# Moving a convolution-weight transform from the head of a kernel to beside its first attention

## The chip, the cores and the metric

The kernel runs on one core of a Trainium2 chip. The metric is the device time of one execution in microseconds (us). The profile is one execution recorded by the hardware profiler; "the trace" is the record of its single instructions. TensorE does matrix products (PE in the profile; PEld is its weight load), VectorE is DVE, ScalarE is ACT, GpSimd is POOL, and SyncE (SP) here only issues transfers.

## The reference, cut to what matters

The program is two layers on four images of 128 channels and 64x64 pixels ("sequences" of 4096 positions). Only the first layer is touched by the change:

```python
x = x + conv_block(group_norm(x))        # first layer
# conv_block(x) = relu(conv7(x) + conv5(x) + conv3(x) + nonlocal(x) + x), all fp32
# nonlocal: theta, phi, g = three 1x1 projections; softmax(theta^T phi / 8) applied to g; 1x1 projection
# second layer: a two-directional state-space block and a recurrence on 4 x 4096 tokens (untouched)
```

The three convolutions and the identity are merged into one 7x7 kernel, which is brought into a form with fewer products: each of the seven kernel rows is turned into ten 128x128 matrices ("the transform", tensor `u`), and the padded image `xp` into matching combinations of every fourth column ("strips", tensors `f` and `x`).

## The kernel before: the parts that matter

```python
def conv_attention(nc, tc, k, a, t, dmax, B, H, W):
    ...
    for h in range(2):                      # small weights, behind the whole input on SyncE's queue
        nc.sync.dma_start(tw2[:, h, :], a["tpw"][:, 0:IC]); ...      # pw2, tb2, ow2
    nc.sync.dma_start(gw, a["gwt"]); nc.sync.dma_start(gb, a["gb"])
    for i, name in enumerate(("b7", "b5", "b3", "ob")):
        nc.sync.dma_start(bias[:, i : i + 1], a[name])
    ...
    nc.vector.tensor_reduce(bsum, bias, AX.X, ALU.add)               # the bias sum
    with tc.tile_pool(name="l0_ws", bufs=2) as ws:
        for y in range(7):
            conv_weights(nc, ws, k, a, u, y)                         # the transform, row by row
    fp = ctx.enter_context(tc.tile_pool(name="l0_fir", bufs=2))      # the strips take its space
    for b in range(B):
        # statistics of the sequence (st), group norm (pm, gm, dm, qv, pv, ve, rs), normed image xp
        # projections theta, phi, gT
        # attention: 128 steps of two score matmuls (pf), exponential (ex), den += ex, two value matmuls (acc)
        # convolution: strips f and x from xp, products with u
        ...

def load():                                 # whole sequences
    for b in range(B):
        nc.sync.dma_start(t[:, b * T : (b + 1) * T], a["x"][b].rearrange("c h w -> c (h w)"))
```

The framework that builds the program ("the build" below) does not keep the source's order on an engine: an instruction may be put into an earlier gap, as the strips in the prediction's last lines of VectorE are.

Of the kernel before, what the change touches and what calls it, by code (L numbers as in the profile page):

```python
# [15 lines left out]
P = 128  # L16
# [6 lines left out]
IC = 64  # L23
# [72 lines left out]
def conv_attention(nc, tc, k, a, t, dmax, B, H, W):  # L96
# [18 lines left out]
    with ExitStack() as ctx:  # L115
# [10 lines left out]
        bsum = wp.tile([P, 1], F32, name="bsum")  # L126
        for h in range(2):
            half = slice(h * IC, (h + 1) * IC)
            nc.sync.dma_start(tw2[:, h, :], a["tpw"][:, 0:IC])
            nc.sync.dma_start(pw2[:, h, :], a["tpw"][:, IC:P])  # L130
            nc.sync.dma_start(tb2[half], a["tb"])
            nc.sync.dma_start(ow2[half], a["owt"])
        tw2, pw2 = (w.rearrange("p h c -> p (h c)") for w in (tw2, pw2))
        nc.sync.dma_start(gw, a["gwt"])
        nc.sync.dma_start(gb, a["gb"])
        for i, name in enumerate(("b7", "b5", "b3", "ob")):
            nc.sync.dma_start(bias[:, i : i + 1], a[name])
        wk = ctx.enter_context(tc.tile_pool(name="l0_wk", bufs=2))
        xpp = ctx.enter_context(tc.tile_pool(name="l0_xp", bufs=1))
        big = ctx.enter_context(tc.tile_pool(name="l0_big", bufs=1))  # L140
# [7 lines left out]
        nc.tensor.matmul(pgb, ow2[0:IC], gb, start=True, stop=True)  # L148
        nc.vector.tensor_tensor(bsum, bsum, pgb, ALU.add)

        with tc.tile_pool(name="l0_ws", bufs=2) as ws:
            for y in range(7):
                conv_weights(nc, ws, k, a, u, y)
        fp = ctx.enter_context(tc.tile_pool(name="l0_fir", bufs=2))
        xtp = ctx.enter_context(tc.tile_pool(name="l0_pt", bufs=4))

        pe = InOrder(tc, nc.tensor)
        for b in range(B):
# [112 lines left out]
                        divide(q - 1)  # L271
            divide(NQ - 1)


            att = theta.rearrange("p (r w) -> p r w", w=W)

# [72 lines left out]
    return c  # L349


def conv_weights(nc, ws, k, a, u, y):

    w = ws.tile([P, 7, P], F32, tag="w", name="w")
    nc.scalar.dma_start(w, a["w7t"][:, y * 7 : (y + 1) * 7, :])
    for n in (5, 3):
        m = (7 - n) // 2
        if m <= y < 7 - m:
            v = ws.tile([P, n, P], F32, tag=f"v{n}", name="v")
            nc.scalar.dma_start(v, a[f"w{n}t"][:, (y - m) * n : (y - m + 1) * n, :])  # L360
            nc.vector.tensor_tensor(w[:, m : 7 - m, :], w[:, m : 7 - m, :], v, ALU.add)
    if y == 3:

        nc.vector.scalar_tensor_tensor(w[:, 3, :], k.ident, 2.0, w[:, 3, :], ALU.mult, ALU.add)
    nc.vector.tensor_scalar(u[:, 0, y, :], w[:, 0, :], 1.0 / poly(POINTS)[0], None, ALU.mult)
    nc.vector.tensor_copy(u[:, 1, y, :], w[:, 6, :])
    for n, p in enumerate(POINTS):
        c = 0.5 / p**2
        for r in POINTS[:n] + POINTS[n + 1 :]:
            c /= p**2 - r**2  # L370
        part = []
        for odd in range(2):
            s = ws.tile([P, P], F32, tag=f"s{odd}", name="s")
            nc.vector.tensor_scalar(s, w[:, odd, :], c * p**odd, None, ALU.mult)
            for j in range(odd + 2, 7, 2):
                nc.vector.scalar_tensor_tensor(s, w[:, j, :], c * p**j, s, ALU.mult, ALU.add)
            part.append(s)
        nc.vector.tensor_tensor(u[:, 2 + 2 * n, y, :], part[0], part[1], ALU.add)
        nc.vector.tensor_tensor(u[:, 3 + 2 * n, y, :], part[0], part[1], ALU.subtract)


def conv_attention_general(nc, tc, k, a, t, B, H, W):
# [760 lines left out]
@with_exitstack  # L1143
def kernel(ctx: ExitStack, tc: tile.TileContext, a: dict, out: bass.AP):
    nc = tc.nc
    B, C, H, W = out.shape
    T = H * W
    cpool = ctx.enter_context(tc.tile_pool(name="const", bufs=1))
    t = cpool.tile([P, B * T], F32, name="t")
    o = out.rearrange("b c h w -> c b (h w)")  # L1150

    def load():
        for b in range(B):
            nc.sync.dma_start(t[:, b * T : (b + 1) * T], a["x"][b].rearrange("c h w -> c (h w)"))

    load()
    k = Consts(nc, cpool)
    dmax = cpool.tile([P, B * (T // NC)], F32, name="dmax")
    flags = cpool.tile([P, 2], F32, name="flags")
    conv_attention(nc, tc, k, a, t, dmax, B, H, W)  # L1160
    nc.vector.tensor_reduce(flags[:, 0:1], dmax, AX.X, ALU.max)
    nc.vector.tensor_scalar(flags[:, 0:1], flags[:, 0:1], DEN_MAX, None, ALU.is_gt)
    mamba(nc, tc, k, a, t, B, T)
    recurrence(nc, tc, k, a, t, flags[:, 1:2], o, B, T)

    n = cpool.tile([1, 1], mybir.dt.int32, name="nflags")
    with tc.tile_pool(name="ps_flags", bufs=1, space=PSUM) as ps:
        pn = ps.tile([1, 2], F32, name="pflags")
        nc.tensor.matmul(pn, k.ones[:, 0:1], flags, start=True, stop=True)
        nf = cpool.tile([1, 1], F32, name="nf")  # L1170
        nc.vector.tensor_reduce(nf, pn, AX.X, ALU.add)
        nc.vector.tensor_copy(n, nf)
    again = nc.values_load(n[0:1, 0:1], min_val=0, max_val=2 * P, skip_runtime_bounds_check_because="a count of flags")
    with tc.If(again > 0):
        load()
        conv_attention_general(nc, tc, k, a, t, B, H, W)
        mamba(nc, tc, k, a, t, B, T)
        recurrence(nc, tc, k, a, t, None, o, B, T)
# [42 lines left out]
```

## Time and profile before

| | us |
|---|---|
| median of three runs (lowest, highest) | 3421.4 (3418.4, 3432.1) |
| first score matmul (the attention of sequence 1 begins) | 115.0 |
| end of the first attention (first product of the convolution) | 366.9 |
| first score matmul of sequence 2 | 545.2 |

The first stage, up to the second sequence's first score, can be read from single instructions; the rest of the program (2864 to 2882 us in the traces here) is the same code in every kernel below and merely starts earlier or later. The lines of the profile on which the argument rests are in the prediction.

### The profile page before, as it was taken

The numbers are of one execution on the slowest core, as the hardware profiler recorded it, in microseconds if no ns is written. First come the engines' busy times: TensorE is split into PE (matmuls) and PEld (weight loads), VectorE is DVE, ScalarE is ACT, GpSimd is POOL, SyncE is SP. The second block draws the span as 40 slices with busy tenths as digits, with TensorE's granted clock in tenths as the row PEclk, the third lists the DMA queues.
The fourth block names the chain that finished last, engine by engine and source line by source line (L and its number), as shares of the span: only waits on it lengthen the run. The fifth ranks groups of instructions, "written<-read, shape, count | busy, mean of one in ns | idle before, by whom it ended". The sixth has DMA issues, their size and how long they took to land.

```text
span 3409.2 us, 44429 instructions
## 1 busy us (share of the span) xinstructions
PE 2991.7 (88%) x16048; PEld 1445.4 (42%) x16048; DVE 2708.1 (79%) x4682; ACT 1726.3 (51%) x3047; POOL 529.2 (16%) x735
## 2 busy tenths in 40 slices
PE   0899998999989999899996888888888898888776
PEld 0233343333433334233343555555555565555446
DVE  8977858778587785877856998899889988898755
ACT  0445204452045420344204777677777767777454
POOL 0000000000000000000000443244324332334310
PEclk9999999999999999999996999999999999999888
DMA  4000000000000000000002332333233233333002
GB/s 165 1 1 1 0 1 1 1 1 0 0 1 1 1 0 0 1 1 1 0 0 52 77 82 75 78 75 84 67 80 80 76 75 78 84 81 78 2 1 101
DMA packets 72437, 128.21 MB, mean 38 GB/s; under 512 B 16912, under 2 KB 20240, under 8 KB 71184
## 3 DMA queue, kind: packets, MB, share of 16 engines
q1 hardware_dynamic: 65664, 115.63, 13.0%
q10 hardware_dynamic: 6544, 9.65, 0.8%
q8 instruction: 129, 2.11, 0.3%
q14 instruction: 100, 0.82, 0.1%
HBM read 115.80 MB, written 9.44 MB: 37 GB/s over the span
## 4 chain that ended last, share of the span: by engine, by line
PE 57%; DVE 27%; ACT 5%; issue 4%; POOL 3%; DMA 2%; SPq 0%; ACTq 0%; DVEq 0%; POOLq 0%
PE pf L91 14%; PE acc L91 13%; PE pr L286 11%; DVE xx L754 5%; PE pc L286 3%; DVE bc L754 3%; DVE cbc L840 2%; ACT xx L91 2%; DVE y L877 2%; DVE f L298 2%; DVE xdt L833 2%; DVE xdd L833 2%; PE pj L892 1%; POOL xx L91 1%; PE pys L857 1%
## 5 line engine op out<-in xcount | busy, mean ns | idle before, releaser
L233 ACT ACTIVATE ex<-pf 128x1024 f32<-128x1024 f32 x512 | 496.7, 1021 | 495.8 <-PE pf L91 487.3
L237 DVE TENSOR_TENSOR den<-den,ex 128x1024 f32<-128x1024 f32 x448 | 547.1, 1221 | 209.5 <-ACT ex L233 184.7
L91 PE MATMUL pf<-theta,phi 64*128 64x512 f32 x2048 | 509.3, 615 | 1.8 <-ACT ex L233 1.8
L91 PE MATMUL acc<-ex,gT 128*64 128x512 f32 x2048 | 501.2, 606 | 0.0
L286 PE MATMUL pr<-x,u 128*128 128x512 f32 x896 | 386.3, 593 | 0.0
L91 PEld LDWEIGHTS pf<-theta,phi 64*128 64x128 f32 x2048 | 175.7, 186 | 328.4 <-ACT ex L233 186.8
L91 ACT ACTIVATE cbc<-cbc,s 128x128 f32<-128x128 f32 x1024 | 312.9, 406 | 0.0
L91 PEld LDWEIGHTS acc<-ex,gT 128*64 128x64 f32 x2048 | 121.9, 136 | 344.8 <-issue 343.7
L286 PEld LDWEIGHTS pr<-x,u 128*128 128x128 f32 x896 | 170.0, 190 | 219.3 <-issue 216.0
L754 DVE SCALAR_TENSOR_TENSOR xx<-pj,cw,xx 128x509 f32<-128x509 f32 (+2 forms) x384 | 259.6, 735 | 0.4
L857 PE MATMUL pys<-cbc,xdt 128*64 128x128 f32 x2048 | 180.5, 296 | 81.7 <-DVE y L877 81.6
L91 POOL TENSOR_TENSOR rms<-rms,neghalf 128x2 f32<-128x2 f32 x128 | 113.3, 885 | 569.7 <-DVE rms L903 569.7
L327 ACT COPY m<-pr 128x512 f32<-128x512 f32 x32 | 18.8, 586 | 356.5 <-PE pr L286 356.5
L91 ACT ACTIVATE cbc<-cbc 128x1536 f32<-128x1536 f32 x128 | 190.0, 1485 | 3.4
L298 DVE SCALAR_TENSOR_TENSOR f<-xp,f 128x1120 f32<-128x1120 f32 x88 | 190.7, 2180 | 1.0
L91 POOL TENSOR_TENSOR y<-y,zs 128x512 f32<-128x512 f32 x128 | 163.4, 1276 | 147.0 <-DVE y L877 144.5
L857 PEld LDWEIGHTS pys<-cbc,xdt 128*64 128x64 f32 x2048 | 115.9, 142 | 145.1 <-DVE y L877 110.6
L745 PE MATMUL pj<-un,full 128*128 128x512 f32 x256 | 147.4, 661 | 33.8 <-DVE xx L754 19.5
L767 PE MATMUL pj<-un,full 128*128 128x512 f32 x256 | 146.0, 677 | 32.9 <-DVE xx L754 18.0
L91 ACT ACTIVATE xx<-pj,cb,cw 128x512 f32<-128x512 f32 x128 | 97.6, 774 | 144.9 <-DVE y L877 104.9
L892 PEld LDWEIGHTS pj<-wout,y 128*128 128x128 f32 x1024 | 133.4, 199 | 59.1 <-issue 48.5
L181 POOL MEMSET xp<- 128x210 f32 x4 | 1.1, 274 | 1011.4 <-DVE f L298 1011.4
(210 smaller groups left out, 4991.1 us busy)
## 6 DMA issues: line engine op xcount, KB each, us to landing
cbc<-csd SPq DMA_DIRECT2D x256, 256.0 KB, 4.4
cbc<-csd SPq DMA_DIRECT2D x256, 128.0 KB, 4.5
t<-in_x SPq DMA_DIRECT2D x4, 2048.0 KB, 11.8
out<-t SPq DMA_DIRECT2D x2, 2048.0 KB, 18.5
out<-t ACTq DMA_DIRECT2D x2, 2048.0 KB, 18.8
w<-in_w7t ACTq DMA_DIRECT2D x7, 448.0 KB, 8.5
v<-in_w5t ACTq DMA_DIRECT2D x5, 320.0 KB, 14.3
csd<-cs SPq DMA_DIRECT2D x16, 64.0 KB, 1.6
```

What stands on the lines that cost most here:

```text
L91: return self.tc.keep_in_program_order(getattr(self.engine, name)(*args, **kw))
L233: nc.scalar.activation(ex, pf, AF.Exp, scale=scale)
L237: nc.vector.tensor_tensor(den[q], exs[q, 0] if m == 1 else den[q], ex, ALU.add)
L286: nc.tensor.matmul(o, u[:, n, y, :], x[:, q * QR + y : q * QR + y + QR, :], start=(y == 0), stop=(y == 6 and odd is None),)
L298: nc.vector.scalar_tensor_tensor(f, strip(i + 2 * j), cs[j], f, ALU.mult, ALU.add)
L745: pe.matmul(pp, full[:, d, DI + h * P : DI + (h + 1) * P], own(un, d, g), start=True, stop=True)
L754: vec.scalar_tensor_tensor(x[:, o:], self.pp[i][:, 0 : MG - o], cw[:, i, tap : tap + 1], x[:, o:], ALU.mult, ALU.add)
L767: pe.matmul(pz, full[:, d, h * P : (h + 1) * P], cols, start=True, stop=True)
L833: vec.tensor_tensor(x, px, self.r[f][:, :, self.c, :].unsqueeze(3).to_broadcast(heads), ALU.mult)
L840: vec.tensor_tensor(self.lt, self.lt, self.gm.unsqueeze(2).to_broadcast([P, ND, NHEAD, P]), ALU.mult)
L857: pe.matmul(o, self.xdt[:, d, h, :], self.lt[:, d, h, :], start=True, stop=S is None)
L892: pe.matmul(po[:, bass.ts(d, P)], self.y[:, d, h, :], wout[:, d, h, :], start=(h == 0), stop=(h == 1))
```

## The change

Its intent: no work on the weights before the first attention, the first sequence visible to VectorE in quarters, and the transform in the space that the strips take afterwards, in VectorE's free time during the attention. The core of the diff:

```diff
-            nc.sync.dma_start(tw2[:, h, :], a["tpw"][:, 0:IC])
+            nc.scalar.dma_start(tw2[:, h, :], a["tpw"][:, 0:IC])
 ...                                         # the same for pw2, tb2, ow2, gw, gb and the four biases
-        with tc.tile_pool(name="l0_ws", bufs=2) as ws:
-            for y in range(7):
-                conv_weights(nc, ws, k, a, u, y)
-        fp = ctx.enter_context(tc.tile_pool(name="l0_fir", bufs=2))
 ...                                         # after the attention's last step, in the loop over sequences:
+            if b == 0:
+                with tc.tile_pool(name="l0_ws", bufs=1) as ws:
+                    for y in range(0, 7, 2):
+                        conv_weights(nc, ws, k, a, u, y, min(y + 2, 7))
+                fp = ctx.enter_context(tc.tile_pool(name="l0_fir", bufs=2))
 ...                                         # conv_weights: two rows per instruction, loads on SyncE's queue,
-    nc.vector.tensor_scalar(u[:, 0, y, :], w[:, 0, :], 1.0 / poly(POINTS)[0], None, ALU.mult)
+    nc.scalar.mul(u[:, 0, ys, :], w[:, :, 0, :], 1.0 / poly(POINTS)[0])
 ...                                         # (and the other scalings and copies) on ScalarE
-            nc.sync.dma_start(t[:, b * T : (b + 1) * T], a["x"][b].rearrange("c h w -> c (h w)"))
+            n = T // (4 if b == 0 else 1)
+            for i in range(0, T, n):
+                nc.sync.dma_start(t[:, b * T + i : b * T + i + n], x[:, i : i + n])
```

More of the change, by code (lines that the diff above doesn't have):

```diff
@@ L128, in conv_attention @@
             half = slice(h * IC, (h + 1) * IC)
-            nc.sync.dma_start(tw2[:, h, :], a["tpw"][:, 0:IC])
-            nc.sync.dma_start(pw2[:, h, :], a["tpw"][:, IC:P])
-            nc.sync.dma_start(tb2[half], a["tb"])
-            nc.sync.dma_start(ow2[half], a["owt"])
+            nc.scalar.dma_start(tw2[:, h, :], a["tpw"][:, 0:IC])
+            nc.scalar.dma_start(pw2[:, h, :], a["tpw"][:, IC:P])
+            nc.scalar.dma_start(tb2[half], a["tb"])
+            nc.scalar.dma_start(ow2[half], a["owt"])
         tw2, pw2 = (w.rearrange("p h c -> p (h c)") for w in (tw2, pw2))
-        nc.sync.dma_start(gw, a["gwt"])
-        nc.sync.dma_start(gb, a["gb"])
+        nc.scalar.dma_start(gw, a["gwt"])
+        nc.scalar.dma_start(gb, a["gb"])
         for i, name in enumerate(("b7", "b5", "b3", "ob")):
-            nc.sync.dma_start(bias[:, i : i + 1], a[name])
+            nc.scalar.dma_start(bias[:, i : i + 1], a[name])
         wk = ctx.enter_context(tc.tile_pool(name="l0_wk", bufs=2))
@@ L349, in poly, with conv_weights @@
     return c
-def conv_weights(nc, ws, k, a, u, y):
-    w = ws.tile([P, 7, P], F32, tag="w", name="w")
-    nc.scalar.dma_start(w, a["w7t"][:, y * 7 : (y + 1) * 7, :])
+def conv_weights(nc, ws, k, a, u, y0, y1):
+    R = y1 - y0
+    w = ws.tile([P, R, 7, P], F32, tag="w", name="w")
+    nc.sync.dma_start(w, a["w7t"][:, y0 * 7 : y1 * 7, :].rearrange("i (y x) o -> i y x o", x=7))
     for n in (5, 3):
         m = (7 - n) // 2
-        if m <= y < 7 - m:
-            v = ws.tile([P, n, P], F32, tag=f"v{n}", name="v")
-            nc.scalar.dma_start(v, a[f"w{n}t"][:, (y - m) * n : (y - m + 1) * n, :])
-            nc.vector.tensor_tensor(w[:, m : 7 - m, :], w[:, m : 7 - m, :], v, ALU.add)
-    if y == 3:
-        nc.vector.scalar_tensor_tensor(w[:, 3, :], k.ident, 2.0, w[:, 3, :], ALU.mult, ALU.add)
-    nc.vector.tensor_scalar(u[:, 0, y, :], w[:, 0, :], 1.0 / poly(POINTS)[0], None, ALU.mult)
-    nc.vector.tensor_copy(u[:, 1, y, :], w[:, 6, :])
+        l0, l1 = max(y0, m), min(y1, 7 - m)
+        if l0 < l1:
+            v = ws.tile([P, 2, n, P], F32, tag=f"v{n}", name="v")[:, 0 : l1 - l0]
+            nc.sync.dma_start(v, a[f"w{n}t"][:, (l0 - m) * n : (l1 - m) * n, :].rearrange("i (y x) o -> i y x o", x=n))
+            for l in range(l0, l1):
+                o = w[:, l - y0, m : 7 - m, :]
+                nc.vector.tensor_tensor(o, o, v[:, l - l0], ALU.add)
+    if y0 <= 3 < y1:
+        o = w[:, 3 - y0, 3, :]
+        nc.vector.scalar_tensor_tensor(o, k.ident, 2.0, o, ALU.mult, ALU.add)
+    ys = slice(y0, y1)
+    nc.scalar.mul(u[:, 0, ys, :], w[:, :, 0, :], 1.0 / poly(POINTS)[0])
+    nc.scalar.copy(u[:, 1, ys, :], w[:, :, 6, :])
     for n, p in enumerate(POINTS):
@@ L372, in conv_weights @@
         for odd in range(2):
-            s = ws.tile([P, P], F32, tag=f"s{odd}", name="s")
-            nc.vector.tensor_scalar(s, w[:, odd, :], c * p**odd, None, ALU.mult)
+            s = ws.tile([P, R, P], F32, tag=f"s{odd}", name="s", bufs=2)
+            nc.scalar.mul(s, w[:, :, odd, :], c * p**odd)
             for j in range(odd + 2, 7, 2):
-                nc.vector.scalar_tensor_tensor(s, w[:, j, :], c * p**j, s, ALU.mult, ALU.add)
+                nc.vector.scalar_tensor_tensor(s, w[:, :, j, :], c * p**j, s, ALU.mult, ALU.add)
             part.append(s)
-        nc.vector.tensor_tensor(u[:, 2 + 2 * n, y, :], part[0], part[1], ALU.add)
-        nc.vector.tensor_tensor(u[:, 3 + 2 * n, y, :], part[0], part[1], ALU.subtract)
+        nc.vector.tensor_tensor(u[:, 2 + 2 * n, ys, :], part[0], part[1], ALU.add)
+        nc.vector.tensor_tensor(u[:, 3 + 2 * n, ys, :], part[0], part[1], ALU.subtract)
 def conv_attention_general(nc, tc, k, a, t, B, H, W):
@@ L1153, in load @@
         for b in range(B):
-            nc.sync.dma_start(t[:, b * T : (b + 1) * T], a["x"][b].rearrange("c h w -> c (h w)"))
+            x = a["x"][b].rearrange("c h w -> c (h w)")
+            n = T // (4 if b == 0 else 1)
+            for i in range(0, T, n):
+                nc.sync.dma_start(t[:, b * T + i : b * T + i + n], x[:, i : i + n])
     load()
```

## The prediction

> **What bounds the kernel now.** I read the busy tenths of the page first, then a table of stages (busy time of each engine in chosen stretches), then VectorE's groups and the waits before the first projection, then the instructions there in order of time. The busy tenths show one slice (85 us wide) in which TensorE does nothing, the first, while VectorE is busy and the DMA engines carry the kernel's loads:
>
> ```profile
> PE   0899998999989999899996888888888898888776
> DVE  8977858778587785877856998899889988898755
> DMA  4000000000000000000002332333233233333002
> ```
>
> The table of stages, with one row for the start, one for the first projections, and one each for the first and second attention (columns: the stretch, its length, then busy time and count by engine, granted clock, DMA share, GB/s):
>
> ```profile
> 0.00:82.50 82.50, 2.14 (x8) 1.89 (x9) 67.33 (x303) 1.28 (x1) 4.49 (x21) 1.00 0.46 171
> 82.50:115.00 32.50, 23.19 (x161) 10.02 (x161) 32.42 (x24) 9.27 (x19) 0.00 (x0) 0.95 0.00 1
> 115.00:366.90 251.90, 251.07 (x1042) 76.35 (x1038) 194.76 (x169) 125.01 (x129) 0.00 (x0) 1.00 0.00 1
> 545.20:796.20 251.00, 250.67 (x1041) 76.57 (x1039) 187.04 (x152) 124.68 (x129) 0.00 (x0) 1.00 0.00 1
> ```
>
> So the start is VectorE's (67 of 82.5 us; TensorE 2), the projections are VectorE's too (32.4 of 32.5 us), and an attention is TensorE's, without gaps (251 of 251), with VectorE busy about 75% and ScalarE 50%. What VectorE does at the start is the transform of the convolution weights, which nothing needs before the first convolution at about 367 us. VectorE's groups up to 82.5 us (busy us, mean ns, then idle time before them):
>
> ```profile
> L376 DVE SCALAR_TENSOR_TENSOR s<-w,s 128x128 f32<-128x128 f32 x140 | 32.1, 282 | 0.0
> L374 DVE TENSOR_SCALAR s<-w 128x128 f32<-128x128 f32 x56 | 11.5, 217 | 0.0
> L378 DVE TENSOR_TENSOR u<-s 128x128 f32<-128x128 f32 x28 | 7.9, 282 | 0.0
> L361 DVE TENSOR_TENSOR w<-w,v 128x640 f32<-128x640 f32 x5 | 4.1, 817 | 4.1 <-DMA w<-in_w7t 4.1
> L361 DVE TENSOR_TENSOR w<-w,v 128x384 f32<-128x384 f32 x3 | 1.7, 551 | 0.0
> L365 DVE TENSOR_SCALAR u<-w 128x128 f32<-128x128 f32 x7 | 1.5, 219 | 8.8 <-DMA w<-in_w7t 8.8
> ```
>
> Only after it, at 69.65 us, come the statistics of the first sequence, which head the chain to the attention, although its load has long landed (the four loads take 8.8 to 14.4 us from issue to landing and start at 0.8 us). In order of time on VectorE:
>
> ```profile
> 68.84 0.89 DVE L376 SCALAR_TENSOR_TENSOR s<-w,s 128x128 f32<-128x128 f32 x4
> 69.65 0.68 DVE L162 BATCH_NORM_STATS2 st<-t 128x6 f32<-128x512 f32 x1
> ...
> 70.65 4.83 DVE L162 BATCH_NORM_STATS2 st<-t 128x6 f32<-128x512 f32 x8
> 75.40 0.35 DVE L164 BATCH_NORM_AGGREGATE mv<-st 128x2 f32<-128x48 f32 x1
> ...
> 79.57 2.41 DVE L185 TENSOR_SCALAR xp<-t,gm,rs 128x4096 f32<-128x4096 f32 x1 [0.16 <-POOL rs L80]
> ...
> 82.81 2.18 DVE L296 SCALAR_TENSOR_TENSOR f<-xp 128x1120 f32<-128x1120 f32 x1
> ```
>
> The order on an engine is not the program's: strips f, which the source makes after the attention, stand here among the projections. An instruction that is ready early fills a gap of its engine; after that the order is fixed, and a late operand holds all that follows.
>
> [...] in the first 12 us the input's queue held 70% and the weights' queue 14.5% of the DMA engines, and the DMA engines stay near 430 GB/s up to 25 us. [...] five 128x128 multiply-adds take 1.09 us, 202 ns from start to start, of which 128 elements are 133 ns (817 - 551 = 266 ns for 256 elements, above), so 69 ns are per instruction. [...] in the trace the first pair of projection matmuls takes 2.06 us, later ones 1.14.
>
> **The change, part by part.**
>
> *Removed from the start.* The transform runs from 9.84 to 69.65 us, with the 8.8 us wait for w7 ahead of it. All of it lies on the chain. In its place the chain starts with the sequence itself in quarters. At 430 GB/s its 2.1 MB take 4.9 us; in the trace the DMA engines move their first bytes at 2 us and had carried 2.1 MB by about 7.7 us. I add [...] 0.6 us for the 192 KB of projection weights on ScalarE's queue, hence 9.8 us for the last quarter. The statistics of the first three quarters lie under the load; the last two cost 2 x 0.6 = 1.2 us: aggregation at 11.0 us. From there to xp took 79.57 - 75.40 = 4.2 us, unchanged: xp at 15.2 us instead of 79.6. Gain 64 us without hitches.
>
> *Moved: the strips.* From xp to the first score matmul (115.04 us) took 35.5 us, as VectorE put 2.2 us of strip between the projections' 0.65 us evictions: a period of 2.75 us. The strips' space is now the transform's until it ends, so they leave this stage. TensorE's own period is 1.14 + 1.04 = 2.2 us. Eight of these with some delay by small weight instructions are 20 us, [...] the matmuls of g 4, and xp itself with the way to the first matmul 3: 29 us. Gain 6 us; first score at 15.2 + 29 = 44 us.
>
> *Added on VectorE, beside the attention.* Four calls, three of two kernel rows, one of one. A call has 20 multiply-adds and 8 sums: 28 x (69 + 266) ns = 9.4 us for two rows, 28 x 0.202 = 5.7 for one; with the additions of w5 and w3 (5 x 0.75 + 3 x 0.48 = 5.2 us) and the identity (0.2) this is 39 us, against 54 busy before. 70 small scalings go to ScalarE, as 40 instructions of about 0.4 us (a 512-wide copy takes 587 ns there): 15 us in 125 idle. The strips that were built ahead, 14 x 2.1 = 30 us, follow, and 5 us of the next statistics. Together 74 us; VectorE has 251 x 0.25 = 62 us free in an attention and about 20 - 8 x 0.65 = 15 in the projections. That is 74 into 77: nearly full, but it fits.
>
> *The price of being nearly full.* In the kernel before, the first 20 us of the first attention had VectorE busy 19.9 of 20 us, and TensorE 19.18: 0.8 us lost, 4%. The whole first sequence, attention to attention, took 430.1 us against 428.3 for the next two. If a third to two thirds of the attention run so full, it costs 0.04 x (85 to 170) = 3 to 7 us; I take 5. Strips late for the first convolution: 2 us, since that stage leaves VectorE 45 of 151 us.
>
> *Hitches in the start.* Seven loads of the input and fourteen small ones now stand ahead of the weights; SyncE's own waits before show issues held for an earlier, unrelated load (the third input load waited 14.2 us for w7). The bias loads come last and VectorE's sum over them stands early (it waited 1.0 us before); w for the first call can hardly land before 25 us (8.4 + 1.2 MB at 430 GB/s, from 2 us), and a weight instruction put early into VectorE's or ScalarE's order would hold the norm or the projections until then. I take 4 us of a possible 12.
>
> Sum: 64 + 6 - 5 - 2 - 4 = 59, and a little more for the baseline's own 1.9 us lost in the first attention, which is in the 5: 61 us. 3421.4 - 61 = 3360 us, 1.8% less.
>
> **Rivals.** (1) *A wait takes the place of the transform*: VectorE or ScalarE, in their fixed order, sit before a weight instruction or the bias sum whose load is behind the 8.4 MB of input. For it: the first call's transform waited 8.8 and 4.1 us for w7 even when it was loaded first. Against it: the first weight instruction has hundreds of others it could follow. The whole 12 us, and again some for each of the other calls since w has one buffer now: 3372 to 3380 us. (2) *VectorE becomes the bound of the first attention*: the 74 us don't fit, exponentials wait for sums that release their buffers (8.5 us of such waits in the first attention already, on ScalarE), and the strips are not ready at its end. For it: 97% full on paper. Against it: much of the shortage can go into the convolution. It would cost 15 to 25 us: 3372 to 3382. (3) *Everything hides*: TensorE keeps its 251 us, no hitch: 70 to 72 us, 3350. (4) *The load was hidden anyway*, so quarters are worth nothing: they shorten only the 5 us of statistics; against the 60 us this decides little.
>
> **Range and chances.** (3) gives the lower end, 3346 with some noise; (1) and (2) together rarely in full, 3380. Faster by over 2% means under 3353, over 68 us: only with nearly no hitch, 0.28. Slower is hardly possible, since nothing is added to a stage without room: 0.01.
>
> **What would show it.** Right: the first statistics at about 4 us, xp at 14 to 22 us, the first score at 42 to 52, weights' instructions spread over 25 to 170 us and strips after them, TensorE over 95% busy in the first attention, everything behind shifted by one constant. Wrong: VectorE or ScalarE with long waits for w, v or bias before the first score; waits of the exponentials for den over 20 us; an empty TensorE between the first attention and the convolution; or a sequence of other length than 428 us from the second on.

## More of the kernel before

Only TensorE's attention matmuls are held to the source's order here.

## The result

The changed kernel takes 3406.6 us (median of four runs, 3403.5 to 3409.9). The ratio to the kernel before is 0.9948 with a 95% interval of 0.9924 to 0.9972. Ratios here are the mean time of one kernel's runs over the mean of the other's in the same rounds, so they are not quite the ratio of the medians that are quoted. The forecast of 3360 us and its range from 3346 to 3380 were wrong: some 17 us came instead of 61.

The busy tenths of the changed kernel (40 slices of 85 us). The hole in TensorE's first slice is half filled. The second slice reads 8 as before, but then it held the last 30 us of the start; now it is attention alone, which should fill it. VectorE's fullest early slices are now the second and the third (9 and 8; before, the first and second):

```profile
PE   5899989999899998999986889888988898888776
DVE  6987767778677786877856998898889888898755
```

The stages of the first sequence, read from the single instructions (us):

| | before | after | gain | predicted gain |
|---|---|---|---|---|
| normed image xp begins | 79.6 | 34.0 | 45.6 | 64 less 4 for hitches |
| from xp to the first score matmul | 35.5 | 27.8 | 7.6 | 6 |
| first attention, first score to the convolution's first product | 251.9 | 288.6 | -36.7 | -5 |
| from there to sequence 2's first score | 178.2 | 177.7 | 0.6 | -2 |
| sequence 2's first score matmul | 545.2 | 528.1 | 17.1 | 59 to 61 |

The sum, 17.1, is the difference of the medians too, if the kernel before is taken with all four of its runs of these rounds (3423.7 us; the 3421.4 above is of the first three). The totals of the two traces do not show it: the rest of the program, whose code is the same, took 2864 us in the trace of the kernel before and 2880 in the other, and scatters by 18 us over all the traces. Three terms were about right, and two were not: the start gave 14 us less than predicted, and the attention took back 37 us instead of 5.

**The start.** VectorE in order of time in the changed kernel (start, duration, engine, line, operation, and in brackets the idle time before it and what ended that):

```profile
12.08 0.69 DVE L158 BATCH_NORM_STATS2 st<-t 128x6 f32<-128x512 f32 x1 [1.50 <-DMA t<-in_x]
29.94 0.16 DVE L146 TENSOR_REDUCE bsum<-bias 128x1 f32<-128x4 f32 x1 [17.05 <-DMA bias<-in_ob]
30.01 0.68 DVE L158 BATCH_NORM_STATS2 st<-t 128x6 f32<-128x512 f32 x1
30.73 0.37 DVE L160 BATCH_NORM_AGGREGATE mv<-st 128x2 f32<-128x48 f32 x1
...
33.99 2.42 DVE L181 TENSOR_SCALAR xp<-t,gm,rs 128x4096 f32<-128x4096 f32 x1 [0.76 <-POOL rs L80]
```

The build put the sum over the four biases, which nothing needs before the convolution, ahead of the last statistics instruction. VectorE sat before it for 17 us, with the whole first sequence in place. The load it waited for, 512 bytes for `ob`, was issued at 11.6 us and landed at 29.9. The four bias loads took 7.5, 12.3, 16.7 and 18.3 us, each longer than the one before, while the rest of the input kept the same DMA engines 95% busy (361 GB/s from 8.4 to 29.9 us); in the kernel before, where they came behind the input, they took 2.1 to 3.0 us. This is the prediction's rival 1 in the place that it named, only larger (it had allowed 12 us at most).

**The first attention.** Its stages in the changed kernel (columns as in the prediction's table of stages): the end of the projections, the rest of the transform, the strips, the rest:

```profile
0.00:61.80 61.80, 25.01 (x168) 12.06 (x168) 29.87 (x58) 12.27 (x26) 4.47 (x21) 1.00 0.49 174
61.80:137.70 75.90, 62.30 (x242) 17.93 (x240) 74.65 (x150) 39.72 (x65) 0.00 (x0) 0.96 0.14 44
137.70:184.50 46.80, 35.71 (x120) 9.28 (x116) 46.79 (x29) 14.12 (x14) 0.00 (x0) 0.85 0.00 0
184.50:350.40 165.90, 165.47 (x685) 50.12 (x683) 127.11 (x105) 81.65 (x84) 0.00 (x0) 1.00 0.00 1
```

In the kernel before, one of the attention's 128 exponentials was done every 251.9 / 128 = 1.97 us. Counting them in each stretch gives 30, 14 and 84. So the transform's stretch lost 75.9 - 30 x 1.97 = 16.9 us, the strips' stretch 46.8 - 14 x 1.97 = 19.2 us, and the long rest 0.6 us: together the 36.7. VectorE is 98% to 100% busy in the two bad stretches and leaves 39 of 166 us unused in the good one. It had the time, but later. Fourteen strip instructions stand behind the transform (138 to 182 us), nearly in a row:

```profile
148.46 1.29 DVE L233 TENSOR_TENSOR den<-den,ex 128x1024 f32<-128x1024 f32 x1
149.59 2.24 DVE L301 SCALAR_TENSOR_TENSOR f<-xp,f 128x1120 f32<-128x1120 f32 x1
149.84 1.02 ACT L229 ACTIVATE ex<-pf 128x1024 f32<-128x1024 f32 x1 [4.38 <-DVE den L233]
150.92 2.08 PE L91 MATMUL pf<-theta,phi 64*128 64x512 f32 x4 [2.41 <-ACT ex L229]
151.67 1.29 DVE L233 TENSOR_TENSOR den<-den,ex 128x1024 f32<-128x1024 f32 x1
152.80 2.22 DVE L301 SCALAR_TENSOR_TENSOR f<-xp,f 128x1120 f32<-128x1120 f32 x1
153.05 1.02 ACT L229 ACTIVATE ex<-pf 128x1024 f32<-128x1024 f32 x1 [2.19 <-PE pf L91]
```

One sum and one strip alternate, 3.2 us from sum to sum, where the attention needs a sum every 1.97 us. The exponential waits for the sum that gives its buffer back (4.38 us in the third line), the score matmuls wait for the exponential (2.41 us in the fourth), and TensorE stands.

A part of the loss comes on top of the standing. TensorE's own waits in this attention (total, times, longest) are 25.1 us:

```profile
PE pf L91 <- ACT ex L229: 25.1, 18, 3.1
```

Most of the remaining 11 us is a slower clock in and after such waits. TensorE is busy 62.3 us in the transform's stretch for work that takes 30 x 1.97 = 59.0, and 35.7 us in the strips' stretch for 27.6, at mean granted clocks of 0.96 and 0.85. The trace grants half the clock in four spells, 103.2 to 106.6, 123.6 to 127.1, 151.0 to 157.8 and 168.0 to 174.8 us, 20.5 us together, which can cost some 10 us (an estimate: half of the 20.5). In order of time on TensorE:

```profile
102.25 1.21 PE L91 MATMUL pf<-theta,phi 64*128 64x512 f32 x4 [3.12 <-ACT ex L229]
103.39 3.50 PE L91 MATMUL acc<-ex,gT 128*64 128x512 f32 x8
...
108.74 1.94 PE L91 MATMUL acc<-ex,gT 128*64 128x512 f32 x8
```

Eight matmuls of the same kind take 3.50 us after a wait of 3.12 us, and 1.94 us five microseconds later. In the strips' stretch TensorE waited 7 times, 11.1 us in all and 2.4 us at most, at the mean clock of 0.85. After a wait of 2.21 us, with none in the nearly 8 us before it, half the clock was granted from 123.6 to 127.1 us; after one of 2.17 us, ended at 79.5, it was 1.00. Why the one and not the other is not shown.

ScalarE's waits in the same attention (total, times, longest) show a second candidate. Besides the exponentials it stands before weight instructions, 14.5 us for loads and 13.4 us for VectorE to release a buffer, and in its fixed order the next exponential stands behind them:

```profile
ACT ex L229 <- DVE den L233: 30.6, 13, 4.9
ACT u L374 <- DMA w<-in_w7t: 14.5, 3, 6.3
ACT s L383 <- DVE u L388: 13.4, 9, 3.1
```

So the question for the experiments (the start has its own, e1 and e5): does the attention lose its 37 us to the weight instructions on ScalarE and their late loads (a wait), to a lack of VectorE time (too much work), or only to the places that the work has in VectorE's order?

### The profile page after: what moved, and what is told of

Read it like the earlier page. It is cut to its first block, busy times and chain, and to the rows that moved or that the text cites. A ratio compares the mean times of both kernels' runs of the same rounds, so it can differ in the third digit from the quotient of the medians.

```text
span 3408.1 us, 44290 instructions
## 1 busy us (share of the span) xinstructions
PE 3021.9 (89%) x16048; PEld 1456.4 (43%) x16048; DVE 2692.6 (79%) x4528; ACT 1740.2 (51%) x3087; POOL 528.1 (15%) x735
## 4 chain that ended last, share of the span: by engine, by line
PE 55%; DVE 28%; ACT 5%; issue 4%; POOL 3%; DMA 3%; SPq 0%; ACTq 0%; DVEq 0%; POOLq 0%
PE pf L91 13%; PE acc L91 12%; PE pr L289 11%; DVE xx L763 6%; PE pc L289 3%; DVE bc L763 3%; DVE cbc L849 2%; ACT xx L91 2%; DVE y L886 2%; DVE xdd L842 2%; DVE xdt L842 2%; DMA cbc<-csd 2%; DVE den L233 1%; PE pys L866 1%; PE pj L901 1%
## 5 line engine op out<-in xcount | busy, mean ns | idle before, releaser
L91 PE MATMUL pf<-theta,phi 64*128 64x512 f32 x2048 | 517.3, 622 | 26.1 <-ACT ex L229 26.1
L776 PE MATMUL pj<-un,full 128*128 128x512 f32 x256 | 150.6, 695 | 33.3 <-DVE xx L763 18.3
## 6 DMA issues: line engine op xcount, KB each, us to landing
out<-t ACTq DMA_DIRECT2D x2, 2048.0 KB, 18.3
```

The source lines that it names most:

```text
L91: return self.tc.keep_in_program_order(getattr(self.engine, name)(*args, **kw))
L776: pe.matmul(pz, full[:, d, h * P : (h + 1) * P], cols, start=True, stop=True)
```

## The experiments

All were correct. "First score" and "second score" are the first score matmuls of the sequences 1 and 2, "attention" is the length of the first one, as in the table of stages; edits are against the changed kernel.

| run | first score | attention | second score | ratio to before [95%] | median us |
|---|---|---|---|---|---|
| before | 115.0 | 251.9 | 545.2 | | 3421.4 to 3426.8 |
| after | 61.8 | 288.6 | 528.1 | 0.9948 [0.9924, 0.9972] | 3406.6 |
| e1_bias_first | 43.3 | 288.8 | 509.5 | 0.9889 [0.9862, 0.9917] | 3388.4 |
| e2_strips_spread | 62.2 | 270.4 | 511.7 | 0.9880 [0.9857, 0.9903] | 3387.0 |
| e3_all_vector | 59.5 | 293.9 | 530.8 | 0.9956 [0.9929, 0.9983] | 3409.0 |
| e4_rows_buffered | 58.8 | 293.0 | 529.5 | 0.9959 [0.9931, 0.9987] | 3411.6 |
| e5_rest_later | 47.0 | 288.7 | 513.8 | 0.9899 [0.9881, 0.9917] | 3390.1 |
| e6_loads_only | 111.4 | 256.7 | 545.8 | 0.9995 [0.9979, 1.0012] | 3422.6 |
| e7_spread | 44.5 | 266.0 | 491.4 | 0.9836 [0.9812, 0.9860] | 3364.7 |
| e8_spread_later | 47.0 | 266.1 | 490.7 | 0.9858 [0.9837, 0.9879] | 3373.7 |
| e9_gaps | 46.0 | 254.9 | 479.3 | 0.9799 [0.9780, 0.9817] | 3355.9 |
| e10_gaps_later | 41.7 | 256.9 | 477.3 | 0.9804 [0.9788, 0.9821] | 3358.6 |
| e11_transform_only | 57.4 | 283.8 | 518.9 | 0.9921 [0.9903, 0.9938] | 3399.5 |
| e12_both | 42.3 | 253.1 | 473.8 | 0.9779 [0.9756, 0.9803] | 3351.1 |

### e1: the small loads in another order

The four bias loads go to the head of ScalarE's queue; nothing else changes.

```diff
+for i, name in enumerate(("b7", "b5", "b3", "ob")):
+    nc.scalar.dma_start(bias[:, i : i + 1], a[name])
+nc.scalar.dma_start(gb, a["gb"])
 for h in range(2): ...                      # tw2, pw2, tb2, ow2
 nc.scalar.dma_start(gw, a["gwt"])
-nc.scalar.dma_start(gb, a["gb"])
-for i, name in enumerate(("b7", "b5", "b3", "ob")):
-    nc.scalar.dma_start(bias[:, i : i + 1], a[name])
```

> The changed kernel with one edit: the bias loads and gb are issued first on ScalarE's queue, ow2 next, then tw2, pw2, tb2, gw. Theory (VectorE stands 17.0 us before the bias sum, in its fixed order ahead of the last statistics, while the load of ob lies behind the input): xp starts at about 17 us instead of 34.0, the first score matmul comes at about 45 us instead of 61.8, the attention keeps its length of 288.6 us, and the time falls by 15 to 17 us against the changed kernel, to about 3390. Rival 1 (the other small loads, tw2, pw2 or ow2, now lie behind the input in their place and the wait only changes its name): first score at 55 us or later, less than 7 us gained. Rival 2 (the first attention is bound by when the transform's loads land, about 32 us for the first): first score comes earlier but the attention becomes longer by as much, nothing gained.

Measured: the wait before the bias sum falls from 17.0 to 1.3 us, xp begins at 16.1 us (predicted for the change: 15.2) and the first score at 43.3 (predicted 44). The time falls by 18 us. So the start's sum in the prediction was nearly right for a start without this hitch, and the hitch is one small load. The four bias loads now took 4.4 to 5.3 us; the small loads in their place behind them (`pw2`, `tb2`, `gw`) took 7.5, 9.7 and 12.3 us. Nothing waited for those here; in e9, with the same load order, VectorE waited 2.1 us for `tb2`, and the first score came at 46.0. The attention stays at 288.8 us: the two losses are independent.

### e2: only the strips spread out

`tc.issue_after` fixes a place in an engine's order and adds no wait. From the 48th of the attention's 120 sums on, every fifth now gets one strip instruction behind it.

```diff
-nc.vector.tensor_tensor(den[q], ..., ex, ALU.add)
+dens.append(nc.vector.tensor_tensor(den[q], ..., ex, ALU.add).ins)
 ...                                         # strips of the first sequence, n = 0, 1, ...
-nc.vector.scalar_tensor_tensor(f, ...)
+with tc.issue_after(dens[48 + 5 * n]):
+    nc.vector.scalar_tensor_tensor(f, ...)
```

> The changed kernel with one edit: each of the first sequence's 14 strip instructions that are built ahead is held in VectorE's order behind one given den addition of the attention, one per five additions, from the 49th to the 114th; no wait is added. Theory (the strips cost 19 us because 30 us of them are packed into the 47 us from 138 to 184, where VectorE is full, although it has 25% free later): the stretch of the strips costs below 4 us, attention about 272 us instead of 288.6, time 15 to 19 us less than the changed kernel, near 3390. Rival (VectorE lacks room in the attention as a whole, so what leaves one stretch is lost in another or at the start of the convolution): attention within 5 us of 288, or TensorE waits for strips when the convolution starts, and the time is that of the changed kernel.

Its stages, the transform's stretch and everything from there to the attention's end:

```profile
62.20:138.00 75.80, 63.32 (x240) 17.88 (x238) 74.27 (x149) 39.82 (x65) 0.00 (x0) 0.93 0.14 44
138.00:332.70 194.70, 194.17 (x805) 59.04 (x801) 173.10 (x135) 95.00 (x98) 0.00 (x0) 1.00 0.00 1
```

Measured: the attention falls from 288.6 to 270.4 us. The second stretch holds 98 exponentials in 194.7 us, 1.8 more than 98 x 251.9 / 128, with the same strips in it; TensorE is full at clock 1.00. The transform's stretch is as before the edit (16.8 us lost). So the strips' 19 us were their places, not their amount.

### e3: all of the transform on VectorE

The 70 scalings, 40 instructions in the change, go back to VectorE, so ScalarE has exponentials alone to do.

```diff
-nc.scalar.mul(s, w[:, :, odd, :], c * p**odd)
+nc.vector.tensor_scalar(s, w[:, :, odd, :], c * p**odd, None, ALU.mult)
 ...                                         # the other two the same
```

> The changed kernel with one edit: the transform's 40 scalings and copies run on VectorE instead of ScalarE. ScalarE waited 14.5 us for w's loads and 13.4 us for VectorE to free s, ahead of exponentials in its fixed order; the stretch of the transform costs 16.9 us. Theory (ScalarE's fixed order carries those waits into the exponentials and so to TensorE): these waits vanish, TensorE's loss in the stretch falls to 8 us or less, though VectorE has some 8 to 10 us more work; time 5 to 10 us less than the changed kernel. Rival (VectorE's load alone makes the loss): the stretch becomes longer by the added 8 to 10 us of work, the attention is 295 us or more and the time 5 us more.

ScalarE's waits in its attention:

```profile
ACT ex L229 <- PE pf L91: 86.3, 45, 3.0
ACT ex L229 <- DVE den L233: 78.3, 38, 6.4
```

Measured: ScalarE's 28 us of waits for weights are gone, and the attention is 5 us longer, with VectorE busy for 255 us of it instead of 249. Exponentials now wait 78 us for sums. The theory, that these waits are the cost and their removal gains 5 to 10 us, fell; the rival, VectorE's load in these stretches, is nearer (it had 295 us or more and 5 us more time; 2.4 us more came). The edit does not remove the waits alone, since it gives VectorE 7 us more work, so it does not show that they cost nothing.

### e4: one row per call, with buffers

```diff
-for y in range(0, 7, 2):
-    conv_weights(nc, ws, k, a, u, y, min(y + 2, 7))
+for y in range(7):
+    conv_weights(nc, ws, k, a, u, y, y + 1)
-w = ws.tile([P, R, 7, P], F32, tag="w", name="w")
+w = ws.tile([P, R, 7, P], F32, tag="w", name="w", bufs=3)
 ...                                         # v with bufs=2
```

> The changed kernel with one edit: the transform goes row by row again (7 calls), with three buffers of w and two of each v instead of one, so that loads are issued two rows ahead; ScalarE keeps the scalings. Theory (about half the transform stretch's loss is ScalarE's waits for w, which one buffer puts after the previous call's last reader): the waits for w fall from 14.5 us to under 4, but VectorE's instructions are twice as many and cost 6 us more, and the waits for s stay; the stretch's loss falls from 16.9 to 10 to 14 us, the time by 2 to 6 us. Rival (the loads hardly matter, VectorE's work does): the loss rises by the 6 us of instruction cost, time 3 to 6 us more.

Measured: the waits for `w` fall from 14.5 to 5.8 us, and the attention grows to 293.0 us. Row by row there are more and smaller instructions, so VectorE has more to do (254 us busy in this attention instead of 249). ScalarE's waits before `s`, for VectorE and its buffers, grew meanwhile from 14.0 to 25.9 us, so its waits for weights did not become less in total (31.7 us instead of 28.5). That later loads alone are the cause is thus not supported, but this edit is no clean test of ScalarE's waits either. (Two buffers for two rows each, without smaller instructions, were not run.)

### e5: the other sequences' loads put off

```diff
 def load(first_only=False):
     for b in range(B):
+        if b > 0 and first_only: break
 ...                                         # after the transform's source, for b == 0
+for i in range(1, B):
+    nc.sync.dma_start(t[:, i * T : (i + 1) * T], a["x"][i].rearrange("c h w -> c (h w)"))
```

> The changed kernel with one edit: sequences 1 to 3 of the input are loaded after the weights instead of before them (their loads stand behind the transform's on SyncE's queue); order of the small loads as in the changed kernel. Theory (the ob load took 18.3 us because 6.3 MB of input that nothing needs before some 480 us lay in front; and the transform's first call stood idle until 58 us for the same reason): the wait before the bias sum falls from 17.0 to under 3 us, first score at 43 to 47 us; the first call and part of the second run in VectorE's gaps among the projections, so the attention falls from 288.6 to 275 to 283 us, its strips stretch still costing about 19; time 22 to 30 us under the changed kernel, near 3380. Rival (what makes the small loads slow is something else than the input's volume, such as the number of loads on one queue): the bias wait stays above 8 us.

Measured: the bias sum waits 4.7 us instead of 17.0 (I had expected under 3), and the first score comes at 47.0, as expected. With e1 this shows from two sides what held the start: a small load that stood late in its queue and beside a stream (the four bias loads took 4.4 to 5.3 us in e1, 3.7 to 7.2 here). But the attention was 288.7 us and not 275 to 283. Transform work did move ahead of it (36.5 us of it are left in the attention, 45.9 in the changed kernel), but statistics of the later sequences, whose loads now came later, moved in: 10.2 us instead of 3.4. VectorE is busy 247.5 us of the attention, hardly less than in the changed kernel (248.5), and the strips still stand in a row (120 to 158 us).

### e6: the new loads alone

The change's loads, and the transform of the kernel before at the start.

```diff
+with tc.tile_pool(name="l0_ws", bufs=2) as ws:      # ahead of the loop over sequences
+    for y in range(7):
+        conv_weights(nc, ws, k, a, u, y)            # the form of the kernel before
 ...
-            if b == 0: ...                          # the transform beside the attention
```

> Part one of the change alone: the quarters and the small loads on ScalarE's queue, with the transform row by row in front of the attention, on VectorE, as in the kernel before. Theory (the gain lies in taking the transform out of the chain, not in the loads; with the loads alone w7 now lands behind the input, some 20 us later): no gain, time from that of the kernel before to 15 us more, first score at 115 to 135 us and attention 252 us. Rival (the early first sequence alone is worth something, since the norm can pass the transform in VectorE's order): first score before 100 us, time 15 us or more under the kernel before.

VectorE in order of time:

```profile
5.06 2.72 DVE L162 BATCH_NORM_STATS2 st<-t 128x6 f32<-128x512 f32 x4 [4.00 <-DMA t<-in_x]
...
21.70 0.16 DVE L146 TENSOR_REDUCE bsum<-bias 128x1 f32<-128x4 f32 x1 [9.07 <-DMA v<-in_w5t]
...
23.81 0.22 DVE L366 TENSOR_SCALAR u<-w 128x128 f32<-128x128 f32 x1
```

Measured: ratio 0.9995. The statistics of the first two quarters start at 5 us, but xp begins at 79.59 us as in the kernel before, since the norm still stands behind the transform. The quarters are worth nothing alone, as the prediction's rival 4 had it. First score (111.4) and attention (256.7) each missed the expectation by some 4 us, the first to the good side, the second to the bad.

### e7 and e8: transform and strips in chosen places

Both put each call's four groups of weight instructions (one for each of the four points with its negative, the additions with the first) behind chosen sums and exponentials. e7 keeps e1's load order, e8 has e5's loads.

```diff
+with group(n):        # issue_after(dens[p]) and issue_after(exps[p]) for the place p of group n
     for odd in range(2): ...
```

e7: calls for rows 2, 4 and 6 at sums 8, 13, 18, 23; 28, 33, 38, 43; 48, 51, 54, 57; strips from 62, every fourth. e8: rows 4 and 6 at 8, 13, 18, 23; 28, 31, 34, 37; strips from 42, every fifth; the calls ahead are left to the build.

> The changed kernel with three edits: bias loads first as in e1; strips held one per four additions from the 63rd addition as in e2; and calls 2 to 4 of the transform held in VectorE's and ScalarE's order, one of a call's four points behind every fifth addition (or exponential) from the 9th to the 44th, then every third to the 58th. Call 1 stays free. Theory (the attention's loss is local: both kinds of added work were packed into its first 124 us at 99% of VectorE, with 25% free after it; spread out they fit): first score at 43 to 45 us, attention 255 to 264 us, no stretch of it with TensorE under 93%, time 60 to 68 us under the kernel before, near 3360. Rival (the transform's loss is from its waits on loads and buffers, or from work that VectorE lacks room for however it is placed): attention stays at 270 us or more, or TensorE waits for strips or u at the start of the convolution, time near 3372.

> The changed kernel with e5's edit (sequences 1 to 3 loaded after the weights), strips held one per five additions from the 43rd, and only calls 3 and 4 of the transform held (from the 9th to the 38th addition); calls 1 and 2 free, to fill the projections. Theory (with w landing early, about 20 us of the transform fit into VectorE's gaps before the first score, and the rest has 62 us of room for 47 us of work): first score at 44 to 48 us, attention 253 to 260 us, time 62 to 70 us under the kernel before, 3355 to 3362. Rival (work put among the projections delays the evictions of theta and so the first score by as much as it saves): first score after 50 us, time no better than e7.

Measured: the attention falls to 266.0 and 266.1 us, and the times to 3364.7 and 3373.7. Both miss their expectation for the attention, e7 by 2 us and e8 by 6, and e8 that for the time by 12 us (it had 3355 to 3362). In e7 ScalarE waits 8.9 us for `w`, as calls stand too close for the load between them (loads of `w` took 4.7 us in the median); in e8 the call left to the build crowds the first 37 us (TensorE busy 30.7), and ScalarE waits 8.2 us for `w`. Loads do cost something once VectorE's crowding is gone.

### e9: the same with wider gaps between the calls

```diff
 # places of the groups (index of the sum); strips from 58, every fourth
-2: [8, 13, 18, 23],  4: [28, 33, 38, 43],  6: [48, 51, 54, 57]      # e7
+2: [12, 16, 20, 24], 4: [31, 35, 39, 43],  6: [50, 52, 54, 56]      # e9
 ...                                         # ScalarE's places: exps[p + p // 15 + 1], in e7 exps[p]
```

> e7 with other places: calls 2, 3 and 4 of the transform start 12, 31 and 50 additions into the attention, with room for a load of about 5 us between the last instruction of a call and the first of the next (in e7 ScalarE still waited 8.9 us for w, twice, ahead of exponentials); ScalarE's scalings are held at the exponentials that belong to these additions; strips from the 59th addition, one per four, to the 111th instead of the 115th (in e7 TensorE waited 2.0 us for the last at the convolution's start). Theory (what is left of the loss in e7 is these waits): ScalarE's waits for w under 1 us in the attention, attention 256 to 261 us instead of 266.0, 3 to 9 us less than e7 against the kernel before. Rival (the rest is VectorE's lack of room): 264 us or more, waits of exponentials for den in place of those for w.

Its stages (the two halves of the attention) and ScalarE's waits in it:

```profile
46.00:173.00 127.00, 125.16 (x522) 38.28 (x518) 122.93 (x189) 73.15 (x101) 0.00 (x0) 1.00 0.08 27
173.00:300.90 127.90, 126.10 (x523) 38.19 (x521) 124.15 (x95) 62.81 (x64) 0.00 (x0) 1.00 0.00 1
```

```profile
ACT ex L230 <- PE pf L91: 83.8, 52, 3.0
ACT ex L230 <- DVE den L234: 27.3, 20, 3.0
```

The halves of e1's attention, which has the same loads and the same work, beside it:

```profile
43.34:166.00 122.66, 96.30 (x358) 26.72 (x356) 121.20 (x179) 53.65 (x79) 0.00 (x0) 0.93 0.08 27
166.00:332.10 166.10, 165.67 (x687) 50.10 (x683) 127.28 (x105) 81.64 (x84) 0.00 (x0) 1.00 0.00 1
```

Measured: the attention takes 254.9 us, 3.0 over the kernel before's, and the first stage ends at 479.3. e1 and e9 differ in the order of VectorE and ScalarE alone (both have 114 instructions of the transform, 5 of statistics and 15 of strips on VectorE in the attention), and that order is worth 288.8 - 254.9 = 34 us. In e9 VectorE is 97% busy from end to end and TensorE 99%. In e1 VectorE is 99% busy in the first part and 77% in the second, and TensorE loses the difference. Note that the exponentials wait 27 us for sums in e9 as well (30.6 in the changed kernel), and it costs next to nothing: TensorE itself waits 2.0 us for exponentials, against 25.1, and its granted clock stays 1.00. Nor does the longest of ScalarE's waits tell: it is 3.0 us in e9 and 4.9 in the changed kernel, but 3.9 in the kernel before, where TensorE then waited only 0.4 us.

### e10: e9 with the loads put off

The load order of e1, e5's late loads and places 3, 8, 13, 18 / 25, 30, 35, 40 / 47, 49, 51, 53 with strips from 55.

```diff
-2: [12, 16, 20, 24], 4: [31, 35, 39, 43], 6: [50, 52, 54, 56]       # e9
+2: [3, 8, 13, 18],   4: [25, 30, 35, 40], 6: [47, 49, 51, 53]       # e10
```

> e9's three edits together with e5's (sequences 1 to 3 loaded after the weights); call 1 free among the projections, calls 2 to 4 held from the 4th, 26th and 48th addition, strips from the 56th, one per four. With bias first as well, xp at 16 to 18 us instead of e8's 21.3. Theory (the last local crowding was call 2 in the first 35 us of e8's attention, and the bias wait of 4.5 us): first score at 42 to 45 us, attention 254 to 259 us, 64 to 72 us under the kernel before, about 3356. Rival (the input's later loads or the statistics of the next sequences now collide with something): no better than e9.

Measured: the first score at 41.7 us and the attention at 256.9 as expected, but 2 us longer than in e9, as ScalarE waits 6.5 us for additions into `w` and 1.9 for its load: the calls again stand too close. At 3358.6 us it can't be told from e9 (3355.9; same rounds, overlapping intervals).

### e11: the moved transform alone

The loads of the kernel before (whole sequences, the small weights behind them), with the transform of the change.

```diff
-n = T // (4 if b == 0 else 1)
+n = T
 ...                                         # and the small loads back on SyncE's queue behind them
```

> Part two of the change alone: the transform beside the attention as in the changed kernel, with the loads of the kernel before (the input in four whole sequences on SyncE, the small loads behind them on the same queue, no weights in front any more). Theory (the small loads that the projections, km and the bias sum need lie behind 8.4 MB of input, 20 us or more): xp at 30 to 40 us, first score at 57 to 67 us, attention about 288 us, time within 6 us of the changed kernel, 3402 to 3414; so the quarters and the second queue bring nearly nothing as long as the bias waits. Rival (the quarters bring several us): time 3415 or more, xp after 40 us.

Measured: 3399.5 us, ratio 0.9921, 3 us better than the lower end of what I expected and some 7 us better than the whole change. The traces agree (second score 9 us earlier), though the intervals of the times touch. So all of the change's gain comes from the moved transform, and the new loads, the first part of the change, add nothing in the form that it gave them; they rather cost some. xp begins at 30.8 us; it is held by 24 statistics instructions of the other sequences (14 to 29 us), which stand before the norm in VectorE's order.

### e12: the places of e9, the load order of e1, the late loads of e5

```diff
+ e1's load order, e5's late loads, e9's places
```

> e9's places with e10's loads (bias first, sequences 1 to 3 after the weights). e9 had the shorter attention (254.9 us) but a late first score (46.0 us, with waits for tw2, pw2 and tb2 behind the input); e10 the early first score (41.7) but an attention of 257.9 us, with ScalarE's waits for v and w at calls that were placed too close. Theory (the two are independent): first score at 41 to 43 us, attention 254 to 257 us, the next sequence's first score at 473 to 477 us against 545.2 in the kernel before; time 69 to 75 us under it, near 3352. Rival (the input's later loads delay the transform's by sharing SyncE's queue, so the two can't be had together): attention 258 us or more, time as e9's.

Measured: 3351.1 us (median of five, 3342.2 to 3360.1), ratio 0.9779 [0.9756, 0.9803]: better than both kernels. The first stage ends at 473.8 us, where 473 to 477 were expected, with an attention of 253.1 us, 1.2 over the kernel before's. Against e9 the trace's first stage is 5.6 us shorter and the median 4.8 us lower, but the intervals overlap, so the gain of the late loads on top is not settled by the times.

## Why the prediction was wrong

- **The removed start chain** (64 us): right as a chain, and e1 shows its end to be nearly right (16.1 us against 15.2). A part of that is luck: in e1 the aggregation starts at 12.9 us, not at 11.0 (the last quarter lands at 11.4 instead of 9.8; what its 9.8 holds beyond 7.7 us for the bytes and 0.6 for the weights was an estimate of mine that no trace gave), and from there to xp it takes 3.2 us, not 4.2. The change itself has xp at 34.0.
- **Hitches in the start** (4 of a possible 12 us): mis-sized. It was a single hitch of 17 us, the bias sum's wait. The prediction had named the bias loads as last and the sum as early, and then put the wait at a third of its worst case. The worst case itself was too small: it thought of the loads' place in the queue, while most of the wait was the 18.3 us that the last of the four 512-byte loads took beside the stream of input (the four took 7.5 to 18.3). That cost 14 us of the forecast.
- **The moved strips** (6 us): right, 7.6. **Strips late for the convolution** (2 us): not seen, the stage gained 0.6.
- **The work added to the attention** (74 us into 77 free): right as a sum. e9 does that work in an attention of 254.9 us, with VectorE 97% busy.
- **The price of being nearly full** (5 us): this is the step that failed, with 36.7 us measured. It took one stretch's rate, 4%, for a VectorE that is full on average, and multiplied it by the length. But nothing spreads the work. In the traces the build packed it as early as it was ready, so for 123 us VectorE had more than the attention could bear (22% lost in the transform's stretch, 41% in the strips'), and for 166 us it had a quarter of its time unused. The prediction knew the rule ("an instruction that is ready early fills a gap") and did not apply it to the work that it was moving. In a better order 5 us are enough: 3.0 in e9, 1.2 in e12.
- **Rivals.** (1) came true in the start, larger than its limit. (2) gave the right picture, exponentials waiting and VectorE the bound, for a reason that e9 contradicts: the work does fit. (4) holds in e6, where the transform still stands in front; what the quarters are worth once it has moved is not measured alone. The sign that the prediction named for (2), waits for sums of over 20 us, was a bad one, since e9 has 27 us of them at a loss of 3; the other sign, TensorE over 95% busy, told (263 of 289 us, 91%, in the changed kernel; 99% in e9).
- **Readings that do not hold.** The prediction has the first pair of projection matmuls at 2.06 us and later ones at 1.14. The third `pt` pair, after a wait of 2.80 us, took 1.71, at a granted clock of 0.50 from 93.0 to 96.4 us: half the clock after a wait could be seen in the kernel before. The first two pairs took 2.06 and 1.91 us, the next two 1.14 and 1.04, so 1.8 us more, but at a granted clock of 1.00 from 82.5 to 86.0 us: why they took longer is not shown. The prediction's 29 us from xp to the first score hold 2 us for them, beside 20, 4 and 3. And the DMA engines moved 427 GB/s from 8 to 12 us but 404 from 12 to 25, not near 430.

**What stays open.** Why the build orders the work as it does is not shown here, only that it does. How much of the 17 us of the transform's stretch is VectorE's crowding and how much ScalarE's waits between calls is not separated beyond this: removing ScalarE's waits at the price of 7 us of VectorE work gained nothing (e3), and spreading alone left some 11 us to gain by wider gaps and later places on ScalarE (e7 to e9).

## What to carry to other kernels

Free time of an engine, summed over a stage, says what can fit; whether it fits was decided here by the places of the added work in that engine's fixed order (288.8 us in e1, 254.9 in e9, with the same work and the same loads), so spread it by hand at the rate that the bound engine leaves (here one strip for every four or five sums) and judge it by the waits of the bound engine itself (here TensorE's 25.1 and 2.0 us), not by those of the engines that feed it. Before a bulk load is moved, look for tiny loads behind or beside it and for the first instruction on each engine that waits for one (here 512 bytes that took 18.3 us, and a wait of 17.05 us). Test the parts of a change alone: here one part carried all the gain, and the other helped only with its small loads in another order (second score at 509.5 us in e1, 518.9 in e11; the intervals of the times overlap).
